# Small SBUF-to-SBUF gathers moved from SyncE's DMA queue to GpSimd's, at another step, in a convolution and attention kernel

## The chip, the cores and the metric

The kernel runs on one core of a Trainium2 chip. The metric is the device time of one execution in microseconds (us), as the median of several runs. Five engines work side by side on their own instruction streams: PE (TensorE, matmuls), DVE (VectorE), ACT (ScalarE), POOL (GpSimd) and SP (SyncE, which here only issues DMAs).

## The reference

The input `x` is (4, 384, 48, 48) in float32: 4 images, 384 channels, 2304 tokens each.

```python
local = conv_general_dilated(x, conv_w, SAME, feature_group_count=C)   # 7x7, one filter a channel
local = local * inv + (bn_beta - bn_mean * inv)                        # batch norm
x_norm = layernorm(x_flat)                                             # over the channels of a token
q, k, v = (x_norm @ qkv_w.T + qkv_b) split into 8 heads of 48
q = q + layernorm(local_flat)
attn = softmax(q k^T * 48**-0.5)
out = x_flat + (attn v) @ proj_w.T + proj_b
```

## The kernel before, in words

**Tiling.** Channels lie on the 128 partitions in three chunks; 2 heads make a pair, 4 pairs p = 0 to 3. An image's queries are cut into five groups (8, 10, 10, 10, 10 rows of 48 tokens, so 384 or 480 columns), which gives 20 groups t = 0 to 19; g = t mod 5 is the group's place in its image. For each group and pair, `score` (L1150) multiplies 18 blocks of 128 keys with the queries, ScalarE takes the exponential (L1158), and `weigh` (L1165) multiplies with the values and, in one more row, with ones, so that row 48 of each head holds the softmax's denominator. At the start of each image there is a stretch that makes keys, values and queries of the whole image (from L1344 on).

**Layout, and why there are tails.** A pair's two heads stand at partitions 0 to 47 and 64 to 111. The first three pairs p = 0, 1, 2 use the head of a chunk; the fourth pair's 48 channels a head are spread as "tails" of 16 rows over partitions 48 to 63 and 112 to 127 of the three chunks. So the fourth pair needs two movements across partitions, each by small DMAs inside SBUF:
- `gather_tails(t)` (L732) collects the query tails of `xn` into the tile `qt`: 8 DMAs of 16 partitions (L739), read by `high_queries(t, 3)` (L1006) and `low_queries(t, 3)` (L1011).
- `tails_out()` (L1065) takes the finished sums of the fourth pair of the group before, in the tile `aot`, back to the tails of `ao`: 6 DMAs (L1070). It runs after `sums_add` (L1049), which makes the last addition on VectorE (L1056) and writes the denominators to memory (`den`, L1061).

`qt` and `aot` are the same buffer (tag "qt", one of it), so the gathers of a group can go only when the copies of the group before have landed.

**Order of the work.** A group is worked in slots: 12 slots of 6 key blocks for t = 0 to 3, 10 slots of 7 or 8 for the others. A slot has four stages, and `here(name)` is true where `PLACES_12` or `PLACES_10` give (slot, stage) for that name; in this way each side task has a place written by hand. In each slot `score_batch` comes first, then `weigh_batch`, and between them VectorE's convolution taps (L351), of which `spare` and `plan` give each point a share. PE, DVE, ACT and SP run in the order in which the program states their instructions; POOL's order is set by the scheduler of the language layer.

**What the steps below touch.**
- `Norm.out` (L672) writes partial sums of a layer norm over channels to memory and reads them back in another shape (`parts`, L682; `four`, L683), both on SP; `few_centre` (L692 to L700) and the squares on ScalarE (L597) need them.
- `low_queries` (L1008) subtracts on VectorE (L1011) and then issues 6 DMAs on SP (L1016, L1018), 4 for the fourth pair.
- `divide` (L1080) reads the denominators (`rd`, L1077) on SP, inverts them on VectorE (L1087), writes them (L1092) and broadcasts them (L1097, L1100); `tensor_mul` by `rb` (L1485) and `hold` (L1117, on POOL) follow at the place "multiply".
- `load_keys` (L805) brings one of 12 stacks of 6 key blocks (768 KB) on POOL into one of three buffers. A load waits until PE has done with the stack that lies in the buffer. In the text "key load n" of a group is that of its stack n, counted from 0.
- `sums_out` (L1047) copies sums from PSUM on ScalarE, so that PE can use the bank again.

The places that matter, as (slot, stage): in 12 slots divide (2, 0), tails (0, 1), multiply (7, 3), fourth pair's queries read at slot 6; in 10 slots divide (1, 1), tails (2, 1), q_sum (2, 3), q_centre (4, 1), multiply (5, 1), fourth pair's queries read at slot 4.

Of the kernel before, what the change touches and what calls it, by code (L numbers as in the profile page):

```python
# [26 lines left out]
PLACES_12 = {  # L27
    "x_sum": (2, 3), "x_centre": (4, 3), "x_squares": (5, 0), "x_sum_squares": (5, 3),
    "x_variance": (7, 0), "x_root": (7, 1), "x_scale": (8, 0),
    "divide": (2, 0), "tails": (0, 1), "multiply": (7, 3), "fetch": (8, 0),  # L30
}
PLACES_10 = {
    "x_sum": (1, 3), "x_centre": (3, 1), "x_squares": (3, 1), "x_sum_squares": (3, 3),
    "x_variance": (5, 1), "x_root": (5, 1), "x_scale": (5, 3),
    "divide": (1, 1), "tails": (2, 1), "multiply": (5, 1), "fetch": (7, 0),
    "q_sum": (2, 3), "q_centre": (4, 1), "q_squares": (4, 1), "q_sum_squares": (4, 3),
    "q_variance": (6, 1), "q_root": (6, 1), "q_end": (6, 3), "q_high": (6, 3), "q_low": (7, 3),
}
# [21 lines left out]
def unshifted_pass(  # L60
# [16 lines left out]
    nc = tc.nc  # L77
# [23 lines left out]
    def columns_of(t):  # L101
        return size(tokens[t % NA])
# [32 lines left out]
    def load_x(b, g, queue=nc.gpsimd):  # L135
        load_packed(place_x(b, g), x[b, :, g * G : (g + 1) * G], queue)
# [355 lines left out]
    def later(b):  # L492

        return X_LATER + (b == 1)
# [58 lines left out]
    def convolve(*point, at=0, then=None):  # L553
        nonlocal made
        for _ in range(share[point]):
            if then is not None and made >= at:
                then()
                then = None
            next(stream)
            made += 1  # L560
        if then is not None:
            assert made >= at
            then()
# [168 lines left out]
    def gather_tails(t):  # L732

        src = queries[t][0]
        dst = work.tile([P, GM], F32, tag="qt", name=f"qt{t}", bufs=1)[:, : columns_of(t)]
        queries[t] = src, dst
        for i, c in enumerate((*range(CC), 0)):
            for r in (0, 64):
                nc.sync.dma_start(  # L739
                    out=dst[r + 16 * i : r + 16 * i + 16], in_=src[r + HD : r + 64, c, :]  # L740
                )

# [55 lines left out]
    def keep_stack(b, i):  # L798
        at = slice(i * third, (i + 1) * third)
        nc.gpsimd.dma_start(out=wide[b, 0][:, :, at], in_=stacks[b, 0, i].bitcast(F32))  # L800
# [81 lines left out]
    def both(making):  # L882
        next(making)
        next(making)
        while soon:
            soon.popleft()()

    def lows_out(n):
        for _ in range(n):
            lows.popleft()()  # L890
# [88 lines left out]
    def local_end(t, rs):  # L979
        acc = accs[t]  # L980
        nc.vector.scalar_tensor_tensor(acc, acc, -1.0, rs, ALU.mult, ALU.mult)
# [67 lines left out]
    def sums_add():  # L1049

        if not parts_of:
            return
        t, p, last, part = parts_of.popleft()
        dst = partial(t, p)[0 : 64 + HA]
        ao, ao3, den = outputs[t]
        nc.vector.tensor_add(dst, dst, part[0 : 64 + HA])  # L1056
        if not last:
            return
        for j in range(2):
            r = 64 * j  # L1060
            nc.sync.dma_start(out=den[2 * p + j : 2 * p + j + 1], in_=dst[r + HD : r + HA])  # L1061
        if p == NP - 1:
            tails_of.append((ao, ao3))

    def tails_out():  # L1065
        while tails_of:
            ao, ao3 = tails_of.pop()
            for c in range(CC):
                for r in (0, 64):
                    nc.sync.dma_start(  # L1070
                        out=ao[r + HD : r + 64, c, :], in_=ao3[r + 16 * c : r + 16 * c + 16]
                    )

    def sums_in(t):
        few = NH * columns_of(t) // P
        rd = work.tile([P, NH * GM // P], F32, tag="rd", name="rd")[:, :few]
        nc.sync.dma_start(out=rd, in_=outputs[t][2].rearrange("h (k f) -> (h k) f", f=few))  # L1077
        return rd

    def divide(t, rd=None):  # L1080

        n = columns_of(t)
        few = NH * n // P
        rd = sums_in(t) if rd is None else rd
        rb = work.tile([P, CC, GM], F32, tag="rb", name="rb", bufs=1)[:, :, :n]
        rden = dram.tile([NH, n], F32, tag=f"rden{n}", name=f"rden{t}")
        nc.vector.reciprocal(rd, rd)  # L1087

        for bound, op in ((SAFE, ALU.is_le), (1 / SAFE, ALU.is_ge)):
            held_in = inside[:, :few]  # L1090
            nc.vector.scalar_tensor_tensor(held_in, rd, bound, held_in, op, ALU.mult)
        nc.sync.dma_start(out=rden.rearrange("h (k f) -> (h k) f", f=few), in_=rd)  # L1092
        heads = rden[0:6].rearrange("(c h) n -> h c n", h=2)
        for j in range(2):
            r = 64 * j
            last = rden[6 + j : 7 + j].rearrange("o (x n) -> o x n", x=1)
            nc.sync.dma_start(  # L1097
                out=rb[r : r + HD], in_=heads[j : j + 1].to_broadcast([HD, CC, n])
            )
            nc.sync.dma_start(out=rb[r + HD : r + 64], in_=last.to_broadcast([16, CC, n]))  # L1100
        return rb
# [3 lines left out]
    def load_residual(b, i, tag="qs", bufs=5):  # L1105
        at = pieces_out[i]
        xr = work.tile([P, CC, GM], F32, tag=tag, name=f"xr{b}_{i}", bufs=bufs)[:, :, : size(at)]
        nc.gpsimd.dma_start(out=xr, in_=x[b, :, at].rearrange("(c p) n -> p c n", p=P))
        residuals[b, i] = xr
# [232 lines left out]
    for t in range(NT):  # L1342
        b, g = divmod(t, NA)
        if g == 0 and b:  # L1344

            sums_add()
            tails_out()
            load_x(b, NG - 1)
            norms_x = {}
            for gk in range(NG):  # L1350
                before = b - 1, gk
                load_residual(*before)
                making = from_x(b, gk, before, ao if gk < NG - 1 else outputs[t - 1][0])
                if gk in (3, 5):
                    keep_stack(b, gk // 2 - 1)
                new = NG - later(b) + gk if gk < later(b) else None
                old = norms_x.get(gk - 1)
                both(making)
                convolve("kv", t, gk, 0)
                if gk == 0:  # L1360
                    rd = sums_in(t - 1)
                if new is not None:
                    norms_x[gk] = Norm(xn[b, new])
                    norms_x[gk].sum()
                    norms_x[gk].out()
                if gk == 4:
                    norm = Norm(accs[t])
                    norm.sum()
                    norm.out()
                both(making)  # L1370
                if old:
                    old.few_variance()
                    old.few_root()
                if gk == 1:
                    rb = divide(t - 1, rd)
                if gk == 5:
                    norm.few_variance()
                    norm.few_root()
                if gk == 2:
                    last_ao = outputs[t - 1][0]  # L1380
                    nc.vector.tensor_mul(last_ao, last_ao, rb)
                convolve("kv", t, gk, 1)
                if gk == 5:
                    local_end(t, norm.few_newton())
                    query_end(t, True)
                both(making)
                convolve("kv", t, gk, 2)
                if gk == 5:
                    low_queries(t, 0)
                lows_out(1)  # L1390
                if new is not None:
                    norms_x[gk].few_centre()
                    norms_x[gk].squares()
                if gk == 4:
                    norm.few_centre()
                    norm.squares()
                both(making)
                convolve("kv", t, gk, 3)
                lows_out(2)
                if old:  # L1400
                    old.scale(old.few_newton())
                both(making)
                convolve("kv", t, gk, 4)
                if new is not None:
                    norms_x[gk].sum_squares()
                    norms_x[gk].out()
                if gk == 4:
                    norm.sum_squares()
                    norm.out()
                both(making)  # L1410
                if gk < NG - 2:
                    ao = fetch(b - 1, gk + 1)
# [147 lines left out]
            steps()  # L1560

    sums_add()
    tails_out()
    for i, at in enumerate(pieces_out):
        ao, n = aos[i], size(at)
        if i == 3:
# [554 lines left out]
```

## Time and profile before

| what | us |
|---|---|
| runs | 2782.07, 2783.0, 2792.41 |
| median | 2783.0 |
| the profiled execution | 2782.09 |
| its span, first to last instruction | 2780.3 |
| PE busy (matmuls) | 2724.7 |
| DVE busy | 2314.3 |
| ACT busy | 1660.0 |
| mean granted PE clock | 0.991 of full |
| gathers L739 on SP: 160 issues, median each | 0.589 |
| copies L1070 on SP: 120 issues, median each | 0.587 |
| key loads L805: from issue to landing, median | 5.2 |

PE's busy time is the sum of the times in which a matmul runs, whether at full clock or not. Of a DMA the profile has two times: that of its issue on the engine that asks for it, and that of its landing, which its semaphore tells. A wait is listed as "who waited <- what ended the wait: us in total, times, the longest". The chain of waits is followed back from the end: each step is what released the one after it.

### The profile page before, as it was taken

What the parts mean: (1) busy time and instruction counts of PE and PEld (TensorE: products, weight loads), DVE (VectorE), ACT (ScalarE), POOL (GpSimd) and SP (SyncE); (2) the same over time, 40 slices, a digit from 0 to 9 for tenths busy, and PEclk for the clock granted to TensorE, in tenths of its full rate; (3) what the DMA queues carried; (4) which work ended last, traced back from release to release, by engine and by line L of the source; (5) the groups of instructions that cost most, each with busy time, mean ns of one, the idle gap of its engine ahead of it and who ended that gap; (6) DMA issues with size and microseconds to landing.
All of it is one profiled execution on the core that took longest, in us unless ns stands there. A gap on an engine that the chain in (4) does not pass through costs nothing.

```text
span 2780.3 us, 45929 instructions
## 1 busy us (share of the span) xinstructions
PE 2724.7 (98%) x16438; PEld 1546.1 (56%) x16438; DVE 2314.3 (83%) x4038; ACT 1660.0 (60%) x2317; POOL 605.5 (22%) x1083
## 2 busy tenths in 40 slices
PE   8999999999999999989999999998999999999999
PEld 5565555555556655545556665554555665555555
DVE  7999989889988998869899889887899888986202
ACT  4356767677325776666732577776762377766662
POOL 5531101102453111010246211101115501111110
PEclk9999999999999999999999999999999999999999
DMA  8454534446455444354645544544545545444442
GB/s 166 89 143 133 133 108 137 115 125 186 100 145 163 121 134 133 100 128 122 177 105 144 174 132 123 147 112 132 139 126 157 137 141 142 127 136 134 135 148 78
DMA packets 159453, 370.45 MB, mean 133 GB/s; under 512 B 58672, under 2 KB 107472, under 8 KB 159216
## 3 DMA queue, kind: packets, MB, share of 16 engines
q0 software_dynamic: 72288, 283.76, 36.1%
q1 hardware_dynamic: 83248, 78.33, 12.3%
q10 hardware_dynamic: 3680, 5.34, 0.6%
q8 instruction: 132, 2.16, 0.3%
q14 instruction: 105, 0.86, 0.1%
HBM read 258.14 MB, written 64.14 MB: 116 GB/s over the span
## 4 chain that ended last, share of the span: by engine, by line
PE 77%; DVE 12%; DMA 6%; SPq 2%; ACT 1%; issue 1%; ACTq 0%; POOL 0%; DVEq 0%
PE o L1165 34%; PE r L1150 28%; PE r L730 15%; DVE acc L351 8%; DMA parts<-part 2%; DMA four<-parts 1%; DMA ao<-aot 1%; SPq L1018 1%; DMA rd<-den 1%; DMA staged<-in_qkv_wT_dram 1%; DMA wide<-k 0%; SPq L1070 0%; DVE k L843 0%; DMA xn<-in_x_dram 0%; ACT pt L1158 0%
## 5 line engine op out<-in xcount | busy, mean ns | idle before, releaser
L351 DVE SCALAR_TENSOR_TENSOR acc<-slab,vec,acc 128x470 f32<-128x470 f32 (+10 forms) x2832 | 1656.1, 657 | 0.3 <-ACT acc L314 0.3
L1158 ACT ACTIVATE pt<-r 128x960 f32<-128x960 f32 (+1 forms) x1440 | 1237.3, 949 | 180.5 <-PE o L1165 97.0
L1165 PE MATMUL o<-pt,v 128*64 128x480 f32 (+1 forms) x5760 | 1162.1, 555 | 0.4 <-ACT pt L1158 0.4
L1150 PE MATMUL r<-qs,ks 64*128 64x480 f32 (+1 forms) x8640 | 976.0, 376 | 34.1 <-ACT o L1047 29.3
L1150 PEld LDWEIGHTS r<-qs,ks 64*128 64x128 f32 x8640 | 790.8, 186 | 288.4 <-issue 146.3
L1165 PEld LDWEIGHTS o<-pt,v 128*64 128x64 f32 x5760 | 397.3, 137 | 668.4 <-issue 576.4
L805 POOL DMA_DIRECT2D ks<-wide x226 | 164.2, 727 | 1233.2 <-PE r L1150 1216.6
L730 PE MATMUL r<-xn,w_qk 128*128 128x384 f32 x864 | 285.2, 487 | 0.0
L1047 ACT COPY o<-o 113x480 f32<-113x480 f32 (+1 forms) x160 | 86.9, 543 | 297.9 <-PE o L1165 264.3
L730 PEld LDWEIGHTS r<-xn,w_qk 128*128 128x128 f32 x864 | 164.6, 191 | 115.6 <-issue 2.3
L730 PE MATMUL r<-w_v,xn 128*128 128x384 f32 x432 | 148.4, 496 | 3.4 <-DVE xn L725 3.3
L827 ACT COPY v<-r 128x384 f32<-128x384 f32 x72 | 32.0, 480 | 191.6 <-PE r L730 191.6
L1056 DVE TENSOR_TENSOR ao<-ao,o 113x480 f32<-113x480 f32 (+1 forms) x120 | 75.9, 633 | 73.9 <-ACT o L1047 73.9
L730 PEld LDWEIGHTS r<-w_v,xn 128*128 128x128 f32 x432 | 82.7, 193 | 64.5 <-issue 5.7
L1047 ACT COPY ao<-o 113x480 f32<-113x480 f32 (+1 forms) x60 | 32.7, 544 | 125.3 <-PE o L1165 125.3
L790 POOL DMA_DIRECT2D wide<-k x144 | 71.8, 500 | 89.5 <-ACT k L840 62.6
L730 PE MATMUL r<-af,w_o 128*128 128x384 f32 (+1 forms) x270 | 85.5, 470 | 2.6 <-DVE k L843 2.6
L125 POOL DMA_DIRECT2D xn<-in_x_dram x72 | 39.7, 554 | 174.8 <-DVE qs L1011 103.4
L857 ACT ACTIVATE xn<-r,qkb 128x384 f32<-128x384 f32 x72 | 40.2, 576 | 56.9 <-PE r L730 53.6
L692 DVE TENSOR_REDUCE few<-four 128x12 f32<-128x48 f32 (+1 forms) x66 | 15.6, 237 | 67.6 <-DMA four<-parts 67.5
L1131 DVE SCALAR_TENSOR_TENSOR xr<-r,pb,xr 128x384 f32<-128x384 f32 (+2 forms) x72 | 42.1, 612 | 35.8 <-PE r L730 27.4
L730 PEld LDWEIGHTS r<-af,w_o 128*128 128x128 f32 x270 | 51.2, 190 | 34.9 <-DVE k L843 3.0
(148 smaller groups left out, 1357.4 us busy)
## 6 DMA issues: line engine op xcount, KB each, us to landing
ks<-wide POOLq DMA_DIRECT2D x226, 768.0 KB, 5.2
qs<-qs SPq DMA_DIRECT2D x352, 60.0 KB
slab<-in_x_dram POOLq DMA_DIRECT2D x24, 432.0 KB, 8.6
wide<-k POOLq DMA_DIRECT2D x96, 96.0 KB, 2.1
wide<-ks POOLq DMA_DIRECT2D x12, 768.0 KB, 5.1
xr<-in_x_dram POOLq DMA_DIRECT2D x16, 576.0 KB, 5.7
rb<-rden SPq DMA_DIRECT2D x32, 270.0 KB
held<-ao POOLq DMA_DIRECT2D x12, 720.0 KB, 4.0
```

The costliest lines, as they stand in the source:

```text
L125: queue.dma_start(out=dst[p0 : p0 + piece.shape[0]], in_=piece)
L351: nc.vector.scalar_tensor_tensor(dst, src, weight, dst, ALU.mult, ALU.add)
L730: nc.tensor.matmul(dst, lhsT=weights(c), rhs=src(c), start=c == 0, stop=c == CC - 1)
L790: nc.gpsimd.dma_start(out=last[16 * u : 16 * u + 16, 0], in_=k[r : r + 16, 0])
L805: queue.dma_start(out=place_keys(b, p, i), in_=wide[b, p][:, :, at])
L857: nc.scalar.activation(src[:, i, :], q[:, :G], AF.Identity, bias=qkb[:, 0, i : i + 1])
L1047: nc.scalar.copy(dst[0 : 64 + HA], sums[0 : 64 + HA, :n])
L1056: nc.vector.tensor_add(dst, dst, part[0 : 64 + HA])
L1131: nc.vector.scalar_tensor_tensor(xr[:, co, :], m, pb[:, co : co + 1], xr[:, co, :], ALU.add, ALU.add)
L1150: nc.tensor.matmul(r[:, j, :n], lhsT=ks[rows, w, at], rhs=qs[rows, m, :], start=i == 0, stop=i == 2,)
L1158: nc.scalar.activation(pt, r[:, :, :n], AF.Exp, scale=SCALE)
L1165: nc.tensor.matmul(sums[halves[j], : columns_of(t)], lhsT=values[t // NA, kb // NB][:, at : at + 64], rhs=pt[:, j, :], start=first, stop=last,
```

## The change

`gather_tails` issues its 8 DMAs on GpSimd's queue in every group. `tails_out` issues its 6 there too, except where it is called outside the groups, at the start of the key stretch of the images 1 to 3 and after the last group: these calls name SyncE. The place "tails" moves from (0, 1) to (2, 3) in groups of 12 slots and from (2, 1) to (1, 3) in groups of 10.

```diff
-    "divide": (2, 0), "tails": (0, 1), "multiply": (7, 3), "fetch": (8, 0),
+    "divide": (2, 0), "tails": (2, 3), "multiply": (7, 3), "fetch": (8, 0),
...
-    "divide": (1, 1), "tails": (2, 1), "multiply": (5, 1), "fetch": (7, 0),
+    "divide": (1, 1), "tails": (1, 3), "multiply": (5, 1), "fetch": (7, 0),
...
         for i, c in enumerate((*range(CC), 0)):
             for r in (0, 64):
-                nc.sync.dma_start(
+                nc.gpsimd.dma_start(
                     out=dst[r + 16 * i : r + 16 * i + 16], in_=src[r + HD : r + 64, c, :]
                 )
...
-    def tails_out():
+    def tails_out(queue=nc.gpsimd):
         while tails_of:
             ao, ao3 = tails_of.pop()
             for c in range(CC):
                 for r in (0, 64):
-                    nc.sync.dma_start(
+                    queue.dma_start(
                         out=ao[r + HD : r + 64, c, :], in_=ao3[r + 16 * c : r + 16 * c + 16]
                     )
...
             sums_add()
-            tails_out()
+            tails_out(nc.sync)
             load_x(b, NG - 1)
...
     sums_add()
-    tails_out()
+    tails_out(nc.sync)
     for i, at in enumerate(pieces_out):
```

So 160 gathers and 96 of the 120 copies change their queue. In the built program the instructions of PE, DVE and ACT stand in the same order as before; SP's are the same without the moved ones. On GpSimd's queue the copies stand around key load 3 of the group and the 8 gathers between them and key load 4; in the first group of an image, the gathers stand between key loads 4 and 5.

## The prediction, as it was put on record

> **What bounds the kernel now.** TensorE does. I read the page's busy shares first, then PE's own waits.
>
> ```profile
> PE 2724.7 (98%) x16438; PEld 1546.1 (56%) x16438; DVE 2314.3 (83%) x4038; ACT 1660.0 (60%) x2317; POOL 605.5 (22%) x1083
> ```
>
> ```profile
> PE r L1150 <- ACT o L1047: 29.3, 6, 8.1
> ```
>
> PE is idle for 2780.3 - 2724.7 = 55.6 us at most, and the largest entry among its waits is 29.3 us in 6 stalls, the score matmuls waiting for ScalarE's copy of finished sums. The remainder lies in the start, the boundary before the second image and the end. So the change can gain only where these stalls are. To place and size them I cut the span at the first exponential of each query group (group 0 to 19) and asked for busy times by window. Columns: window, length, busy time of PE, PEld, DVE, ACT, POOL, granted PE clock, DMA share, GB/s.
>
> ```profile
> 259.90:371.00 111.10, 111.10 (x727) 59.97 (x725) 105.21 (x172) 78.43 (x99) 13.72 (x21) 1.00 0.46 127
> 371.00:488.00 117.00, 113.67 (x728) 60.50 (x726) 106.87 (x175) 78.67 (x99) 13.72 (x21) 0.99 0.44 122
> 488.00:604.30 116.30, 113.22 (x728) 60.33 (x726) 100.00 (x183) 79.95 (x106) 13.73 (x21) 0.99 0.49 126
> 1059.00:1178.70 119.70, 112.50 (x724) 61.06 (x722) 101.66 (x176) 78.46 (x103) 13.72 (x21) 0.96 0.42 120
> 1178.70:1298.20 119.50, 111.42 (x724) 61.33 (x722) 96.62 (x187) 78.33 (x103) 13.73 (x21) 0.96 0.46 124
> 1742.90:1851.40 108.50, 108.50 (x724) 59.93 (x722) 97.25 (x169) 76.68 (x100) 13.59 (x21) 1.00 0.50 140
> 1851.40:1970.80 119.40, 111.81 (x724) 61.41 (x722) 92.92 (x179) 78.33 (x104) 13.73 (x21) 0.96 0.47 124
> ```
>
> Groups 1, 2, 3 (12 slots) do the same matmuls, and so do 7, 8, 12, 13 (10 slots). Group 1 takes 111.1 us and group 12 takes 108.5 with PE never idle. Over those, group 2 loses 5.9, group 3 5.2, group 7 11.2, group 8 11.0, group 13 10.9: together 44.2 us, more than the 29.3 us of idle time in them (window less PE busy). The difference is the clock. After the 8.1 us stall of group 8:
>
> ```profile
> 1242.20:1248.10 5.90, 5.87 (x26) 4.13 (x28) 5.73 (x11) 4.29 (x5) 0.00 (x0) 0.50 0.14 33
> 1248.10:1254.00 5.90, 5.90 (x32) 2.18 (x30) 5.83 (x13) 2.76 (x6) 1.34 (x2) 1.00 0.38 131
> ```
>
> 5.9 us at half the clock do 2.95 us of work: 8.1 + 2.9 = 11.0, which is group 8's loss.
>
> Last, who is late? The chain of waits into that stall (start, us, what):
>
> ```profile
> 1199.39 4.08 DMA parts<-part
> 1203.49 0.59 SPq L683
> ...
> 1207.95 10.16 DMA ao<-aot
> ...
> 1222.91 0.59 SPq L739
> ...
> 1228.06 7.06 DMA parts<-part
> 1235.13 2.29 DMA four<-parts
> 1237.45 0.26 DVE few L692
> 1237.73 0.69 DVE sq L699
> 1238.45 1.67 DVE acc L700
> 1240.65 1.08 ACT sq L597 x2
> 1241.73 0.45 ACT o L1047
> ```
>
> The sums that a layer norm needs (`parts`) stand on SP behind the tails: six copies (L1070), a wait of 10.16 us for the last to land, eight gathers (L739), and six query DMAs. VectorE had made `part` by 1210.3, but SP issued its DMA at 1228.06. VectorE then waited, ScalarE's squares waited for VectorE, and the copy that frees PE's sums stood behind the squares.
>
> ```profile
> DVE few L692 <- DMA four<-parts: 67.5, 21, 14.5
> DVE rd L1087 <- DMA rd<-den: 69.1, 17, 8.4
> ```
>
> ```profile
> SPq L739 <- DMA ao<-aot: 54.3, 27, 9.6
> ```
>
> In groups 2 and 3 the tails stand ahead of the divisors' load (`rd<-den`) instead: VectorE waits up to 8.4 us at L1087, and its additions of sums come late.
>
> **What the Trainium skill says.** "DMA: Bandwidth & Descriptors", section "Anatomy of one DMA": a semaphore wait of a DMA is served on the issuing sequencer, so all behind it on that queue waits; a small DMA costs about 2 us until it has landed. The trace agrees: L739 holds SP until `ao<-aot` has landed, and GpSimd's small `wide<-k` copies land in 1.9 to 2.3 us in the median. Same page, "Issuing engines are not separate DMA queues": another issuing engine saves sequencer time, not transfer time. So I count the bytes at nothing. "TensorE: Matmul & The Clock Gate", "What's actually happening": an idle window of about 3.4 us halves the clock until a busy one has passed; the 0.50 above agrees. "SBUF — State Buffer", "SBUF: two separate sides": some VectorE copies can lock GpSimd out of writing descriptors; here no `wide<-k` issue takes more than 0.58 us beside a VectorE that is 83% busy, so I price that at nothing.
>
> **The change part by part.**
> *Removed from SP:* in each of 16 groups 6 + 8 issues of 0.587 us and about 0.04 between, 14 x 0.63 = 8.8 us, plus the landing wait (1.9 us in group 3, 10.2 in group 8). In the others (0, 5, 10, 15) only the 8 gathers go. What is late next, group by group:
> - Group 8: query DMAs can go when L1011 ends, 1207.6; six take 3.8 us; `parts` goes at 1211.4 instead of 1228.06. Even with the 7.06 us landing and 2.9 for `four`, data is there at 1221.4. VectorE arrives at 1237.4 - 14.5 = 1222.9. No wait left.
> - Group 13: the same from 1880.3 gives 1884.1 instead of 1900.08, 16 us sooner; VectorE waited 13.5 us. No wait left.
> - Group 7: from 1094.1 gives 1097.9 instead of 1108.8, 10.9 us sooner against a wait of 9.7. None left.
> - Group 3: from 499.5, `rd<-den` goes at 503.3 instead of 510.45; with its 4.6 us landing it is there at 507.9, where VectorE arrives at 515.05 - 8.4 = 506.7. A wait of 1.2 is left of 8.4, and PE's stall was 3.08.
> - Group 2: from 383.9, at 387.7 instead of 393.6: 0.6 is left of 6.4, PE's stall was 3.33.
>
> So all five stalls and their slow clock go: -44.2 us. Groups 2 and 3 alone are 11.1, the three others 33.1.
>
> *Added to GpSimd:* 14 issues per group. None of this shape is in the trace there; the nearest rows are `wide<-k` (0.49 to 0.56 us) and `xn<-in_x_dram` (0.55). I take 0.58, 8.1 us a group, on an engine 22% busy whose largest wait is 1216.6 us for PE to release key buffers (L805). Not below nothing: issues on an idle engine can't gain by themselves. The queue order of the built program puts the copies between the group's key loads 2 and 3 and all gathers before load 4. The copies wait for VectorE's last addition. In group 8 that ends at 1182.73, and load 3 goes at 1182.15: new, copies until 1186.2, landing until 1188.5, one gather, load 3 at 1189.1. It lands after the median 5.2 us at 1194.3; its first scores start near 1201.9 (1.3 us before their first exponential). Cover 7.6 us. The other seven gathers end at 1193.9, load 4 goes 1.9 us late and has a cover over 10. Group 7 is the tightest: slab loads go first, three copies stand behind load 3 (which landed 7.7 us after issue), so gathers start near 1078, load 4 goes at 1082.5 and lands by 1089.9; its scores start near 1091.8. Upper bound of this cost is the rival below; I take 1 us in all for the thin cover of group 7.
>
> *Moved:* the program place of `tails` goes from slot 0 to slot 2 (12 slots) and from slot 2 to slot 1 (10). The gathered queries are read at slot 6 or 4 (group 8: 1229.0), 35 us after the gathers' new issue; the copies' reader is the multiplication in slot 7 or 5. Both are hidden; no wait is added there. The removed issues change which SP DMA waits for which earlier one to land; I count nothing for it.
>
> Sum: -44.2 + 1 = -43.2. The profiled execution took 2782.09 us (span 2780.3 and 1.8 around it), 0.9 below the runs' median of 2783.0. The saving comes from the fixed order of the queues, so I take it off the median: 2739.8, say 2740.
>
> **Rivals.**
> 1. *Half of it stays.* The small statistics DMAs may keep landing in 7 us or more because key loads and broadcasts of the divisors fill the DMA engines, or the next DMA on SP may take the tails' place. For: `parts` took 7.06 us with the copies already landed. Against: the arithmetic above already allows for it. If groups 2 and 3 remain, 2751; if two of the long ones remain, 2762.
> 2. *GpSimd becomes the late one (slower).* A copy waits for landing behind a key load, and the next key load stands behind it on the queue. The slowest landing of a small GpSimd copy is 9.97 us (median 2.1): that uses up the 7.6 us cover. Beyond about 10 us PE waits for keys. At 3 us short in each of 16 groups, and 2 us for the clock after it, 16 x 5 = 80: 2740 + 80 = 2820. It turns into a loss from 44 / 16 = 2.8 us a group. Against: the copies move ahead of the divisors' broadcasts, behind which the 10 us landings were seen, and GpSimd already sits up to 22.0 us at the `held` copy (L1117) with key loads behind it and no stall.
> 3. *Nothing moves.* SP is relieved, but VectorE's taps keep it late anyway: 2783. Against: VectorE's waits in the stalled groups exceed PE's stalls.
>
> **How the numbers follow.** All five gone (2732 to 2749): 0.67. The low end allows the boundary stall before the second image (PE idle 5.5 us and half the clock after it) to shrink as well. Part of it (2749 to 2769): 0.16. No effect: 0.08. Slower: 0.09. A change within 0.5% (13.9 us) can't be told from none. Range 2732 to 2763, the first case and most of the second. Faster 0.83, same 0.08, slower 0.09.
>
> **What would show it.** Right: groups 2 and 3 near 111 us and 7, 8, 13 near 108.5, the granted clock 1.00 in them; PE's wait for L1047 near nothing; VectorE's waits for `four` and `rd` far below 67 and 69 us; GpSimd still idle over 1100 us at L805. Wrong: a new row of PE waiting for `ks<-wide`, `ao<-aot` landing over 10 us, or the same stalls with another DMA ahead of `parts`.

## The result, and the profile after

| | median us | runs, us |
|---|---|---|
| before | 2782.53 | 2775.45, 2782.07, 2783.0, 2792.41 |
| after | 2740.14 | 2736.19, 2738.29, 2741.99, 2746.96 |

The ratio is 0.9848, with a 95% interval of 0.9811 to 0.9884: 42 us less, and between 32 and 53 by the interval. The profiled execution of after took 2746.96 us (span 2745.0), the slowest of the four; a second profile of the same kernel comes with the experiments.

First the row of busy shares on the page of after, to be held against 2724.7 us and 55.6 us of idle time before:

```profile
PE 2712.7 (99%) x16438; PEld 1542.5 (56%) x16438; DVE 2312.5 (84%) x4038; ACT 1661.2 (61%) x2317; POOL 732.6 (27%) x1339
```

PE's idle time is now 2745.0 - 2712.7 = 32.3 us, and its busy time is 12 us shorter for the same 16438 matmuls, since less of it ran at half clock. Next the windows of after, cut at the first exponential of groups 1, 2, 3, 7, 8, 12, 13 (columns as before: window, length, PE, PEld, DVE, ACT, POOL, granted clock, DMA share, GB/s):

```profile
259.10:370.00 110.90, 110.90 (x727) 60.04 (x725) 105.15 (x172) 78.51 (x99) 20.65 (x35) 1.00 0.46 127
370.00:481.00 111.00, 111.00 (x728) 60.15 (x726) 106.82 (x176) 78.66 (x100) 20.61 (x35) 1.00 0.46 128
481.00:591.90 110.90, 110.90 (x728) 59.76 (x726) 99.77 (x183) 79.94 (x106) 20.62 (x35) 1.00 0.51 133
1046.40:1154.80 108.40, 108.40 (x724) 59.67 (x722) 101.03 (x175) 78.80 (x103) 20.59 (x35) 1.00 0.49 133
1154.80:1272.70 117.90, 111.60 (x724) 61.06 (x722) 96.19 (x186) 78.40 (x103) 20.64 (x35) 0.96 0.48 125
1717.80:1826.40 108.60, 108.60 (x724) 59.49 (x722) 97.28 (x169) 76.85 (x100) 20.74 (x35) 1.00 0.52 140
1826.40:1934.90 108.50, 108.50 (x724) 59.53 (x722) 92.68 (x179) 78.52 (x104) 20.65 (x35) 1.00 0.53 136
```

Groups 2, 3, 7 and 13 have no idle PE left and run at full clock. Group 8 still has 6.3 us of idle time and a clock of 0.96. POOL has 14 more instructions and about 7 us more in each. The waits of after (who <- what ended it: us in total, times, longest):

```profile
POOL ks L805 <- PE r L1150: 916.4, 151, 10.5
...
POOL ao L1070 <- DVE aot L1056: 132.0, 15, 12.6
...
DVE rd L1087 <- DMA rd<-den: 82.5, 15, 8.7
...
DVE few L692 <- DMA four<-parts: 47.8, 18, 9.0
...
PE r L1150 <- ACT o L1047: 6.3, 1, 6.3
```

PE's 29.3 us in 6 stalls at the copy L1047 are down to one stall of 6.3. There is no row of PE waiting for `ks<-wide`. GpSimd now waits 132.0 us at its first copy for VectorE's last addition, and its wait for PE at L805 fell from 1216.6 to 916.4 us. VectorE's wait for `rd` rose, from 69.1 to 82.5 us. The one stall left, by the chain of waits of after (start, us, what):

```profile
1191.20 18.22 DMA parts<-part
...
1209.43 2.40 DMA four<-parts
...
1211.86 0.26 DVE few L692
1212.12 0.02 issue
1212.14 0.69 DVE sq L699
1212.83 0.02 issue
1212.86 1.67 DVE acc L700
...
1215.06 1.08 ACT sq L597 x2
1216.14 0.45 ACT o L1047
```

No tails stand ahead of `parts` here: SP issued it at 1191.20, when VectorE had just made `part` (1189.6) and the six query DMAs were out. But it took 18.2 us to land, where the forecast had taken 7.06. Columns of the windows around it as above:

```profile
1180.00:1190.00 10.00, 10.00 (x70) 5.59 (x66) 9.86 (x19) 7.32 (x11) 3.30 (x6) 1.00 0.77 185
1190.00:1200.00 10.00, 10.00 (x68) 5.42 (x68) 8.44 (x16) 7.29 (x11) 2.57 (x5) 1.00 1.03 186
1200.00:1210.00 10.00, 10.00 (x64) 4.60 (x60) 2.85 (x6) 4.64 (x6) 0.73 (x1) 1.00 0.82 228
```

The DMA engines were full (1.03) for the first half of that time. In flight were four loads of the slab (issued from 1186.70), a key load (1188.89, landed after 14.5 us) and four image loads into `xn` (1189.63 to 1193.01, landed after 12 to 15 us). Before the change three of those four image loads started from 1226.45 on, 47.7 us into the group instead of 35 to 38. By the profile they waited for SP's transfers of that moment to land; by the code their tokens (1152 to 1535) overlap those of the group (1344 to 1823), which the gathers read, and SP's gathers ended just then.

### The profile page after: what moved, and what is told of

Its sections match the earlier page's. It is cut to its first block, busy times and chain, and to the rows that moved or that the text cites. A ratio compares the mean times of both kernels' runs of the same rounds, so it can differ in the third digit from the quotient of the medians.

```text
span 2745.0 us, 46153 instructions
## 1 busy us (share of the span) xinstructions
PE 2712.7 (99%) x16438; PEld 1542.5 (56%) x16438; DVE 2312.5 (84%) x4038; ACT 1661.2 (61%) x2317; POOL 732.6 (27%) x1339
## 3 DMA queue, kind: packets, MB, share of 16 engines
q1 hardware_dynamic: 75056, 70.80, 11.2%
## 4 chain that ended last, share of the span: by engine, by line
PE 85%; DVE 9%; DMA 4%; issue 1%; ACT 0%; SPq 0%; POOL 0%; DVEq 0%; ACTq 0%
PE o L1165 38%; PE r L1150 32%; PE r L730 15%; DVE acc L351 6%; DMA parts<-part 1%; DMA four<-parts 1%; DMA slab<-in_x_dram 1%; DVE k L843 0%; DMA xn<-in_x_dram 0%; DMA rd<-den 0%; DMA staged<-in_qkv_wT_dram 0%; DVE sq L602 0%; PE r L629 0%; DVE sq L603 0%; DMA wide<-k 0%
## 5 line engine op out<-in xcount | busy, mean ns | idle before, releaser
L1150 PE MATMUL r<-qs,ks 64*128 64x480 f32 (+1 forms) x8640 | 965.7, 374 | 11.1 <-ACT o L1047 6.3
L805 POOL DMA_DIRECT2D ks<-wide x226 | 166.0, 735 | 948.2 <-PE r L1150 916.4
L1047 ACT COPY o<-o 113x480 f32<-113x480 f32 (+1 forms) x160 | 87.1, 544 | 287.3 <-PE o L1165 267.9
L1047 ACT COPY ao<-o 113x480 f32<-113x480 f32 (+1 forms) x60 | 32.7, 545 | 124.9 <-PE o L1165 124.9
L739 POOL DMA_DIRECT2D qt<-xn x160 | 77.3, 497 | 54.2 <-ACT pt L1158 12.9
L1070 POOL DMA_DIRECT2D ao<-aot x96 | 47.3, 498 | 137.4 <-DVE aot L1056 132.0
L1087 DVE RECIPROCAL rd<-rd 128x30 f32<-128x30 f32 (+1 forms) x20 | 6.6, 331 | 82.5 <-DMA rd<-den 82.5
```

What stands on the lines that cost most here:

```text
L739: nc.gpsimd.dma_start(out=dst[r + 16 * i : r + 16 * i + 16], in_=src[r + HD : r + 64, c, :])
L805: queue.dma_start(out=place_keys(b, p, i), in_=wide[b, p][:, :, at])
L1047: nc.scalar.copy(dst[0 : 64 + HA], sums[0 : 64 + HA, :n])
L1070: queue.dma_start(out=ao[r + HD : r + 64, c, :], in_=ao3[r + 16 * c : r + 16 * c + 16])
L1150: nc.tensor.matmul(r[:, j, :n], lhsT=ks[rows, w, at], rhs=qs[rows, m, :], start=i == 0, stop=i == 2,)
```

## The experiments

The theory: the stalls came from what SP had to issue and wait for ahead of the statistics' and the divisors' DMAs, so leaving SP's queue is what helps. Rivals: the place in the program is what helps; the issues alone or the landing wait alone carry it; GpSimd has little room. The leftover of group 8 needs a cause as well.

The table has group lengths in us, cut at the first exponential in each profile (group 4 includes the stretch that starts the second image), and in the last row the landing time of the second `parts` in group 8. e9 is like e7.

| group | before | after | e1 | e2 | e3 | e4 | e5 | e6 | e7 | e8 | e10 | e11 | e12 |
|---|---|---|---|---|---|---|---|---|---|---|---|---|---|
| 2 | 117.0 | 111.0 | 111.0 | 111.0 | 111.0 | 111.0 | 111.0 | 111.5 | 111.0 | 111.0 | 111.0 | 111.0 | 111.0 |
| 3 | 116.3 | 110.9 | 110.9 | 110.9 | 110.9 | 110.9 | 110.9 | 110.9 | 110.9 | 110.9 | 111.5 | 110.9 | 110.9 |
| 4 | 256.8 | 257.5 | 255.1 | 264.5 | 255.9 | 255.8 | 268.0 | 257.4 | 256.4 | 255.0 | 261.6 | 255.1 | 254.5 |
| 6 | 109.4 | 108.5 | 108.7 | 109.3 | 109.0 | 109.7 | 115.6 | 108.5 | 108.5 | 108.6 | 112.8 | 108.5 | 108.5 |
| 7 | 119.7 | 108.5 | 108.6 | 118.8 | 110.2 | 113.1 | 115.3 | 109.3 | 108.5 | 108.8 | 109.9 | 108.5 | 108.4 |
| 8 | 119.5 | 117.9 | 111.2 | 116.3 | 108.5 | 112.4 | 110.3 | 110.9 | 108.5 | 110.3 | 114.2 | 112.3 | 108.5 |
| 11 | 108.5 | 108.8 | 108.7 | 108.5 | 108.5 | 108.5 | 114.9 | 108.5 | 108.5 | 108.6 | 109.8 | 108.8 | 108.4 |
| 13 | 119.4 | 108.4 | 108.4 | 116.9 | 108.5 | 108.5 | 108.6 | 108.4 | 108.4 | 108.5 | 108.5 | 108.5 | 108.5 |
| landing of `parts` | 7.1 | 18.2 | 12.4 | 4.7 | 2.0 | 4.7 | 6.4 | 12.4 | 6.0 | 11.9 | 2.3 | 12.7 | 6.6 |

**e1: the queue alone.** The change with the old places.

```diff
-    "divide": (2, 0), "tails": (2, 3), ...
+    "divide": (2, 0), "tails": (0, 1), ...
...
-    "divide": (1, 1), "tails": (1, 3), ...
+    "divide": (1, 1), "tails": (2, 1), ...
```

> The tails go to GpSimd's queue as in the change, but keep their old places in the program, slot 0 (12 slots) and slot 2 (10 slots). Theory (the queue is what counts: the five stalls come from what SP had ahead of the statistics' and divisors' DMAs): groups 2 and 3 at 111, groups 7 and 13 at 108.5, and a time of 2740 within 5 us, as after the change; group 8, if its leftover of 9 us was an accident of one execution, at 108.5 here. Rival (the place is half of the change: issued later, the copies reach GpSimd behind key load 3 and the key loads come late): 2755 or more, with PE waiting for key buffers.

Measured: 2742.19 us (2741.15 to 2747.74), ratio 0.9871 (0.9836 to 0.9906). The theory holds: groups 2, 3, 7 and 13 as after the change, and no wait for key buffers. The place does nothing here, since the build sets GpSimd's order and gives the same one but for the place of one key load. Group 8 kept 2.7 us: the leftover is smaller than in the profile of after, but it is no accident. It isn't the second `parts` that stalls PE here, though: its stall comes 45.0 us into the group, and that `parts` lands at 48.3 (see e12).

**e2: the place alone.** SP keeps the tails, at the new places.

```diff
-                nc.gpsimd.dma_start(
+                nc.sync.dma_start(
                     out=dst[r + 16 * i : r + 16 * i + 16], ...
...
-    def tails_out(queue=nc.gpsimd):
+    def tails_out(queue=nc.sync):
```

> The tails stay on SP's queue and only their places in the program move. In the 12-slot groups they now stand behind the divisors' DMAs, in the 10-slot groups SP's order is the one of before. Theory: groups 2 and 3 lose their 5.9 and 5.2 us, groups 7, 8 and 13 keep 11 us each, so 2783 - 11 = 2772. Rival (only leaving SP helps): 2783. Rival (an earlier place is what helps the 10-slot groups): 2745 to 2750.

Measured: 2771.28 us (2759.12 to 2783.54 in 22 runs), ratio 0.9967 (0.9953 to 0.9982). The number is the theory's, 2772, but not by its sum alone. Groups 2 and 3 gave 11.4 us as said. Groups 7, 8 and 13 kept 10.3, 7.8 and 8.5 us instead of 11 each, and group 4 lost 7.7 us that it had not lost before. In group 8 `parts` landed in 4.7 us instead of 7.1, though SP's order there is the old one; why isn't shown. The chain of e2 in group 4:

```profile
647.10 4.89 DMA parts<-part
652.00 0.02 issue
652.01 13.81 DMA four<-parts
```

Here `four` took 13.8 us to land, again beside four slab loads, four image loads and three key loads issued within 10 us (644.2 to 653.9). So late landing of a small statistics transfer isn't tied to GpSimd's tails; where it falls differs from version to version.

**e3 and e4: one half on GpSimd.** e3 leaves the six copies on SP, e4 the eight gathers.

```diff
 e3
-    def tails_out(queue=nc.gpsimd):
+    def tails_out(queue=nc.sync):
 e4
-                nc.gpsimd.dma_start(
+                nc.sync.dma_start(
                     out=dst[r + 16 * i : r + 16 * i + 16], ...
```

> New places, but only the eight gathers go to GpSimd; the six copies stay on SP (6 x 0.63 = 3.8 us of issuing, no wait for their landing there). Theory (the wait for landing and the gathers behind it are what held the statistics back): parts of group 8 is issued some 4 us after the queries' DMAs, 14 us sooner than before, so no stall in groups 7 and 13: 2740 to 2746. Rival (each issue on SP costs its share, 3.8 of 18.8 us): 2740 + 0.2 x 43 = 2749. Rival (GpSimd now waits for copies that land late, about 10 us, and key loads behind the gathers come late): over 2760 with PE waiting for key buffers.

Measured: 2741.03 us (2739.77 to 2744.01), ratio 0.986 (0.982 to 0.99). Six issues on SP cost nothing that can be seen in the time, so the first rival falls. The second `parts` of group 8 went at 1197.0 and landed in 2.0 us; GpSimd's gathers came late (from 1197.89), and its image loads behind them (from 1205.79). The second rival shows once: PE waited 1.5 us for a key buffer in group 4.

> New places, but only the six copies go to GpSimd; the eight gathers stay on SP (8 x 0.63 = 5.0 us of issuing), where the copies they wait for have landed long before. Theory: SP loses the wait of up to 10.2 us and the six copies' 3.8 us, so parts goes 13 us sooner than before, against a wait of VectorE of 14.5 us in group 8 and 9.7 in group 7: nothing or 1 to 2 us left of each stall, 2740 to 2748. Rival (issues count as much as the wait, 5.0 of 18.8 us stay): 2752.

Measured: 2749.47 us (2746.94 to 2750.1), ratio 0.989 (0.9849 to 0.993). Groups 7 and 8 keep 4.6 and 3.9 us: the 8.5 us that this kernel lacks. In group 7 `parts` went out 6.0 us after `part` was made, behind the gathers, and then landed in 7.3. The theory had allowed 2 us each. So gathers issued ahead of the statistics do cost, even where the copies have landed before. The halves do not add up: against e2, with the same places, the gathers alone gain 30.2 us and the copies alone 21.8, and both together, at the old places (e1), 29.1. Either move takes the wait for the landing off SP, which is what the two have in common; that wait by itself, without copies or gathers, was not tested.

**e5: all on SP, behind the statistics.**

```diff
-    "divide": (1, 1), "tails": (1, 3), ...
+    "divide": (1, 1), "tails": (2, 3), ...
```
The queues are SP's, as in e2.

> All tails stay on SP, but in the 10-slot groups their place moves a slot later (2, 3), behind the statistics' first DMAs; in the 12-slot groups it is the new one. Theory (what matters is only that nothing slow stands on SP ahead of the statistics' DMAs): the stalls of groups 7, 8, 13 at L1047 go without GpSimd's help. What is late next is the gathers' reader, ScalarE's cast of the fourth pair of queries in slot 4: gathers that now start near 45 us of a group and land 6 us later come up to 6 us after that slot's begin at 42 us, so part of the gain may be given back: 2742 if the cast is hidden, up to 2742 + 13 x 3 = 2780 if every 10-slot group waits there. Rival (GpSimd's early issue is needed): 2775 or more.

Measured: 2767.55 us (2760.94 to 2773.82), ratio 0.995 (0.993 to 0.997). The stalls moved as the theory says. The chain of e5 in group 6:

```profile
996.58 2.99 DMA ao<-aot
999.62 0.51 SPq L739
...
1005.18 1.96 DMA qt<-xn
1007.20 0.06 ACT qs L1006
...
1008.20 1.08 ACT sq L597 x2
1009.28 0.45 ACT o L1047
1009.77 5.06 PE r L1150 x24
```

ScalarE's cast of the fourth pair (L1006) waits for the gathers, and the copy that PE needs stands behind it. Groups 6, 7 and 11 lose 6 to 7 us each in this way, group 13 nothing. Group 4 loses 11, where `four` is late as in e2. Neither place tried on SP is good: ahead of the statistics the tails hold these up, behind them the cast.

**e6 and e10: how much room GpSimd has.** The six copies are issued three and six times over, the same data to the same place.

```diff
-            for c in range(CC):
+            for c in 3 * [*range(CC)] if queue is nc.gpsimd else range(CC):
```
e10 has 6 in place of 3.

> The changed kernel with the six copies issued three times over on GpSimd (the same data to the same place): 12 more issues of 0.49 us, 5.9 us more, ahead of key load 3, in each of 13 ten-slot and 3 twelve-slot groups, and up to 2 x 2.2 us more if a repeated copy has to wait for the one before. This tests the forecast's slower rival. Theory (key load 3 lands 5.6 to 11.5 us ahead of its first exponential, some 1.3 us less ahead of its first scores): 5.9 us is just about covered, and only groups with the thinnest cover (7 by load 4, 5 to 11) lose 1 to 3 us: 2740 to 2755. With 10.3 us of delay 4 us are missing in 10 groups, and the clock's 2 us after each: 2740 + 60 = 2800. In both cases PE waits for key buffers, a row that the changed kernel doesn't have. Rival (GpSimd has more room than that): 2740, no such row.

Measured: 2740.75 us (2736.23 to 2744.59), ratio 0.9864 (0.9844 to 0.9884). The rival is right: 12 more issues in each of 16 groups cost nothing that can be seen. The order of the build changed with them: key load 3 goes after 8 or 9 of the 18 copies in most groups, so only load 4 has less cover (1.1 us ahead of its first exponential in group 4, 1.9 in group 11, over 2.7 elsewhere).

> The changed kernel with the six copies issued six times over on GpSimd (the same data to the same place): 30 more issues of 0.49 us, 14.6 us more in each of 16 groups. With three times over nothing was lost, since the order that the build gives GpSimd lets key load 3 go after 8 or 9 of the 18 copies; load 4 then landed 1.1 to 8.3 us ahead of its first exponential. Here load 4 stands behind 14 to 19 transfers after load 3 instead of 13 or 14, and the rest of copies and gathers goes before load 5. Theory (the cover of the key loads is what decides, and it ends here): load 4 comes 0.5 to 3 us later than with three times over, and load 5 loses 5 to 9 of its 9.8 to 17 us; PE waits for key buffers in groups 4 and 11 and a few others, 1 to 4 us each, 2745 to 2765. Rival (the order adapts again): 2740.

Measured: 2776.31 us (2769.12 to 2783.95), ratio 0.9989 (0.9971 to 1.0008), 34 us above the changed kernel on the same chip (e11). Rows of e10's waits:

```profile
POOL ao L1070 <- DMA ao<-aot: 125.7, 65, 5.4
...
PE r L1150 <- DMA ks<-wide: 23.8, 12, 4.9
```

Now PE waits for key buffers, 12 times, and the whole gain is gone. The theory's mechanism is there, its sum was too small: 2745 to 2765 was expected. Left out was that a repeated copy waits for the one before to land (125.7 us in 65 waits on GpSimd). It was load 5 that came late, landing at most 3.2 us ahead of its first exponential in most of these groups. So the forecast's slower rival is real, but its point lies between 12 and 30 added copies a group, with waits for an earlier copy's landing among them.

**e7 and e12: the divisors' load earlier.** VectorE's wait for `rd` of 8.7 us in group 8 keeps the slab's buffer busy longer (slab loads at 31.9 us of the group, 26.8 before), and so these loads meet the image loads and `parts`. Here the load of the denominators is issued at slot 0, before GpSimd's gathers and key load 3. e12 is the same kernel run again beside e11, the changed kernel.

```diff
+    "sums": (0, 1), ...
...
+            if here("sums") and g:
+                rd_early = sums_in(t - 1)
...
-                rb = divide(t - 1)
+                rb = divide(t - 1, rd_early)
```

> The changed kernel with the divisors' load (rd from den) put at slot 0 instead of beside the division, so that it goes before GpSimd's gathers and key load 3. Theory on group 8's leftover (VectorE waits 8.7 us for rd, which makes the slab's buffer free late, so that slab and image loads, three key loads, the divisors' broadcasts and the statistics come together on the DMA engines): the wait at L1087 falls from 82 us to under 20, the slab loads start 5 us sooner, parts lands in under 8 us, and group 8 takes 108.5: 2730 to 2736 against 2740. Rival (the leftover comes from the image loads alone): rd's wait falls, group 8 keeps 3 to 9 us, time 2740.

> The changed kernel once more, beside the one with the divisors' load at slot 0. Theory: 2740 within 3 us, parts of group 8 landing in 11 us or more again and VectorE waiting 7 to 9 us there at L1087 or L692. Rival (the 18 us were an accident of one execution): landing under 8 us, group 8 at 108.5.

> The kernel with the divisors' load at slot 0 once more, beside the changed kernel. Theory: 2 to 5 us below it, 2735 to 2738, group 8 at 108.5. Rival: no difference.

Measured: e7 2737.63 us (2735.56 to 2739.64), ratio 0.9857 (0.9839 to 0.9875). In one series on one chip: e11 2741.84 us (2740.3 to 2745.68), ratio 0.9872 (0.9847 to 0.9896); e12 2737.11 us (2735.27 to 2741.26), ratio 0.9855 (0.9831 to 0.988). The window of group 8 in e11, then in e12:

```profile
1153.50:1265.70 112.20, 110.41 (x724) 60.71 (x722) 96.19 (x186) 78.45 (x103) 20.61 (x35) 0.98 0.52 132
```

```profile
1153.50:1262.00 108.50, 108.50 (x724) 59.73 (x722) 96.35 (x186) 78.71 (x104) 20.59 (x35) 1.00 0.53 136
```

And VectorE's wait for the divisors, first of e11, then of e12:

```profile
DVE rd L1087 <- DMA rd<-den: 80.7, 15, 8.6
```

```profile
DVE rd L1087 <- DMA rd<-den: 2.7, 2, 1.5
```

The wait is gone, the second `parts` lands in 6.0 and 6.6 us, group 8 has no stall.

Which transfer is late in group 8 differs, though. In the first profile of after and in e6 VectorE waits for the second statistics there, 9.0 and 6.3 us, behind the late `parts`. In e1, e8 and e11 it waits for the first, 5.6 to 5.9 us, and PE stalls 44 to 45 us into the group, before the second `parts` has landed. VectorE's two waits in e11 (in brackets the idle time before, and what ended it):

```profile
1194.47 0.23 DVE L692 TENSOR_REDUCE few<-four 128x12 f32<-128x48 f32 x1 [5.89 <-DMA four<-parts]
1204.64 0.25 DVE L692 TENSOR_REDUCE few<-four 128x15 f32<-128x60 f32 x1 [0.40 <-DMA four<-parts]
```

The first `four` was issued at 1185.09 and took 9.4 us; the second `parts`, at 12.7 us, cost VectorE only 0.4. So the last row of the table explains the stall of after and e6 alone. The early load helps in both cases: in e12 the two `parts` go out 21.0 and 32.9 us into the group, in e11 24.5 and 36.1, since VectorE no longer stands 6.9 us at L1087 ahead of them.

The difference of the medians is 4.7 us, of which group 8 is 3.8; the intervals of the two ratios overlap, so the gain rests on both pairs of profiles rather than on the ratios. With e9 this is the fastest version. What the early load shows is that the leftover follows from the late divisors. It moves the statistics, the broadcasts and the slab loads together, and which of these counts isn't told apart. The order fits the profiles: where the second `parts` goes out ahead of the key load and the image loads, with slab loads in flight, it lands in 6.0 to 6.6 us (group 8 of e7, e9 and e12, group 13 of after); behind the key load and two or three image loads in 11.9 to 18.2 us (group 8 of after, e1, e6, e8 and e11).

**e8 and e9: the image loads moved.** The load of the next image's rows goes to SP, three slots from the end of the group before; e9 has this and the early divisors.

```diff
-            if s == 0 and coming:
-                load_x(b + 1, g - begins(b + 1))
+            if s == n_slots(t) - 3 and next_image and begins(b + 1) - 1 <= g < NA - 1:
+                load_x(b + 1, g + 1 - begins(b + 1), nc.sync)
```

> The changed kernel with the next image's load (four DMAs into xn) taken off GpSimd and issued by SP near the end of the group before, three slots from its end, out of the stretch in which the statistics' sums go out. Theory (parts lands late in group 8, and in group 13 of some runs, because the image loads, let go sooner by the earlier gathers, now share the DMA engines with slab and key loads): parts lands in under 8 us in both, no wait of VectorE over 3 us there, group 8 takes 108.5 to 110: 2732 to 2738. Rival (slab and key loads alone fill the engines): landing stays over 10 us, 2740.

Measured: 2740.03 us (2737.79 to 2745.63), ratio 0.9872 (0.9855 to 0.9889). The landing stayed at 11.9 us (the stall is that of the first statistics), but this doesn't decide for the rival: the edit moved 32 of the 72 loads, and not the one in group 8. That one still went out on GpSimd at 1188.0 us; it comes from the loop at the place "fetch" of the image's last group, from which the build brings it forward. Whether the image loads are needed for the late landing stays open.

> Both: the divisors' load at slot 0 and the next image's load on SP near the end of the group before. Theory (group 8's leftover comes from the divisors' late landing and is gone already with the early load): nothing left to gain from the image loads, 2735 to 2739, the same as with the early load alone. Rival (image loads still cost something in the stretches with statistics): 2 to 4 us below the early load alone.

Measured: 2737.36 us (2736.79 to 2738.3), ratio 0.9855 (0.9828 to 0.9883). The same as the early divisors alone, as the theory says.

## Why the prediction was right

The forecast of 2740 us and its range held, and for the reason that it gave. By its steps:

- **Which stalls, and what they are worth.** Right. The five groups lost 44.2 us over stall-free ones; four of them went to 111.0, 110.9, 108.5 and 108.4, as said. These four gave 6.0 + 5.4 + 11.2 + 11.0 = 33.6 us, where the step counted 44.2 - 11.0 = 33.2.
- **The cause.** Right: the queue (e1), not the place (e2). What the runs show of its parts is that the copies alone on SP cost nothing visible (e3), and the gathers alone, with no wait for a landing ahead of them, 8.5 us (e4). The 12-slot groups alone could also be mended by the place (e2).
- **Group 8.** The term that was mis-sized is "Even with the 7.06 us landing and 2.9 for `four`". The second `parts` went out 36.4 us into the group, where the step has 32.7, as VectorE had stood 8.7 us at the divisors; with the 7.06 us this was still in time (VectorE came at 48.0). But it landed after 18.2 us in the first profile of after, and after 12.4 in e6. The landing in the old profile was carried over, though the change itself sends `parts` off into a fuller stretch. This costs 9.4 us in the slowest run and 2.4 in e6. Left out was the first statistics' `four`, for which VectorE did not wait before: it is what costs 1.8 to 3.8 us in e1, e8 and e11.
- **The divisors.** Wrong: "VectorE's waits for `four` and `rd` far below 67 and 69 us". The wait for `four` fell only to 47.8, and that for `rd` rose to 82.5, since `rd` now lands behind GpSimd's gathers and key load 3, which come at the same time (group 8: issued 1167.50, landed after 8.0 us, beside a key load issued at 1164.83; before, and in e3, where the gathers come later, it landed there after 1.8). PE's time doesn't feel most of it; it makes the leftover in group 8 (e12).
- **GpSimd's cost.** 0.58 us an issue was taken, and 0.49 to 0.50 measured: the rows of after are

```profile
L739 POOL DMA_DIRECT2D qt<-xn x160 | 77.3, 497 | 54.2 <-ACT pt L1158 12.9 <-DMA rd<-den 9.7 <-DMA ao<-aot 8.5
L1070 POOL DMA_DIRECT2D ao<-aot x96 | 47.3, 498 | 137.4 <-DVE aot L1056 132.0 <-DMA slab<-in_x_dram 4.5
```

- The 1 us allowed for the thin cover in group 7 wasn't needed: its load 4 landed at 1076.9, 3.5 us ahead of its first exponential. That "GpSimd still idle over 1100 us at L805" came out as 916 us: of the 300 us less, 132 now stand at the first copy, 127 are GpSimd's added busy time, and the span is 35 shorter.
- **The slower rival** has its mechanism (e10), but its point was set too near: "beyond about 10 us PE waits for keys" took the order of GpSimd's queue as fixed. The build reorders it as the copies grow (e6). The copies also land faster than the 9.97 us taken from the slowest of GpSimd's small copies: in 1.8 us in the median and 6.1 at most in after.
- **The base, and luck.** The forecast took its saving off 2783.0. In longer series the kernel before has medians of 2777.7 to 2781.1 us, and single runs from 2767 to 2796. On one chip the change saves 2777.66 - 2741.84 = 35.8 us, not 43. Of the 7.4 us between, 5.3 are a lower base; the time after is only 2.0 above the forecast (3.8 in group 8, less the 1 us for the thin cover and other small differences). So a saving taken too large and a base taken too high nearly cancel, and that 2740 was met to within a microsecond is in part luck. That the range held isn't.

## What to carry to other kernels

Here SP's queue stood 10.16 us at a landing and held up all that was issued behind it; look at what stands behind such a wait, and not only at the transfer that waits. Before moving such transfers, list what they and their buffers release, since here, with the gathers earlier, image loads went some 10 us sooner, into the stretch where small statistics transfers must land. For those, the landing in the old profile was no bound in the new one; the cure that worked was to issue the small load (the divisors) earlier. Moving the large ones was not tested where it would count. And check in each profile which wait ends last: in group 8 it was not the most striking landing that stalled PE in three of five profiles.

## What the runs showed of the hardware

- The same 16-partition DMA inside SBUF takes 0.59 us to issue on SP and 0.49 to 0.50 us on GpSimd.
- A transfer of 6 to 7.5 KB from SBUF to memory (`parts`) landed in 2.0 us when little was in flight (e3: DMA share 0.08 meanwhile), and in 12 to 18 us when issued behind some 2.2 to 2.4 MB (four slab loads, one key load and two or three of the four image loads, by the sizes of the issues). A full set of DMA engines is not enough for that: in e12 the share was 1.05 while `parts` landed in 6.6 us, and there the key load and the image loads were issued just after it, not before.

```profile
1186.40:1193.00 6.60, 6.60 (x46) 3.42 (x44) 3.88 (x7) 5.80 (x9) 2.93 (x5) 1.00 1.05 203
```

- A stall need not be as long as the 3.4 us that the prediction names for the clock to halve. After the 3.33 us stall of group 2 in before, and after one of 1.79 us in group 8 of e11, 3.4 us ran at about half the clock:

```profile
405.00:408.40 3.40, 3.40 (x12) 1.45 (x14) 3.40 (x6) 2.52 (x4) 0.72 (x1) 0.50 0.20 28
1199.90:1203.30 3.40, 3.40 (x20) 2.72 (x18) 3.33 (x7) 2.95 (x4) 0.00 (x0) 0.51 0.82 242
```

After a stall of 1.7 us in e1 the clock stayed at 1.00. What decides between the two isn't shown.
